# Layer 1 and the FFN read the raw residual; softmax sums are gathered by DMA

## The chip, the cores and the metric

The kernel runs on one core of a Trainium2 chip, as one launch. TensorE (PE, with its weight loads as PEld), VectorE (DVE), ScalarE (ACT), GpSimd (POOL) and the queue of SyncE (SP) work side by side, each on its own list of instructions in order, and wait for one another by semaphores. The metric is the time of the launch on the device in microseconds, as the median of several executions. A profile is one execution.

## What is computed

The input x has 4 images of 128 channels and 64 x 64 pixels, that is 4096 tokens of 128 channels each. Two layers of attention and one recurrent layer (here called the FFN) add to it:

```python
x = x + L0_attention(groupnorm(x))            # q, k of 64 channels, v of 128; softmax over 4096 tokens
t = tokens(x)
t = t + L1_attention(layernorm(t))            # q, k, v of 128; causal; scores * 128**-0.5
t = t + FFN(layernorm(t))
# layernorm(t) = (t - mean) / sqrt(var + 1e-5), over the 128 channels of each token
# FFN: Wx = t @ W.T, normalised per channel over all images and tokens,
#      then y_t = sigmoid(Wx_t + y_{t-1} @ V.T) along the tokens of each image
```

Everything is float32.

## The kernel before

The work is done by `fast_kernel`. (A slower `general_kernel` stands behind it and runs only if a check at the end, written into `wrong`, finds that the recurrence has not converged.) An image is held as X[b], 128 channels on the partitions and 4096 tokens along them. Two of the four images are in SBUF at a time; images 0 and 1 are written to DRAM (`kept`) when they are done and read back at the end.

Attention goes through a list `units`: for each image b, for each layer, for each tile c of 512 queries, for each pair u of key blocks of 128. Layer 0 has 8 tiles of 16 units; layer 1 is causal and has 8 tiles of 2, 4, 6 ... 16 units. `score` (L833) makes the transposed scores `ps` of a unit on TensorE, K blocks as weights, and their exponential `s` on ScalarE (L855 for whole units, L859 for those on the diagonal, which GpSimd then masks, L861). `product` (L867) adds `s` to `total` on VectorE and multiplies it with V on TensorE into `av` (L889). Scores run one unit ahead of products. There are two buffers of `ps`, three of `s`, one of `total`, two of `av`, and two PSUM banks named `misc` for all else.

Around each unit, `step` (L898) advances small generators by one `yield`: all in `ends`, then the first two in `todo`. `whole` runs one to its end where its result is needed.

- `finish` (`e`): after a tile's last unit, the sums in `total` are added, transposed in blocks of 32 and reduced to `part` (128 x 16). A product with `quarters`, `pz`, adds the four quarters of the partitions on TensorE; the reciprocal is spread by a second transpose to `rb`; `o` = `rb` x `av`; `po` = Wv times `o` is added to X.
- `prepare1` (`p1`): layer norm of a tile of 512 tokens for layer 1, in `tokens`: transposed by TensorE, statistics, `rstd` = (var + eps)**-0.5 on GpSimd (L560), then normalised into V1; `back` transposes V1 again into K1, which is both the keys and the source of the queries. `query1` multiplies K1 with M1, a matrix merged from Wq and Wk by `merge1`.
- `ffn` (`f`): the same for the finished residual: `tokens`, `back`, then `pw` = FW times the result, copied into WX, with its statistics in `stats_f`.
- `keys0`, `query0`, `gn_stats`: the inputs of layer 0 for the next image.

`begin_tile` (L796) sets the order: which generators are put into `todo` at which tile, and which are run to their end there. The order within an engine's list isn't always the written one: statistics of image 1 (L595) stand on VectorE from 10.79 us, between steps of image 0, though they are written for the second tile.

After attention, the recurrence runs over 32 positions in 128 chunks at once (L946 to L949), X gets the result on GpSimd (L965), and the images are written out.

Of the kernel before, what the change touches and what calls it, by code (L numbers as in the profile page):

```python
# [472 lines left out]
def fast_kernel(  # L473
# [23 lines left out]

    X = {}

    def load_x(b):  # L500
        X[b] = xpool.tile([P, N], F32, tag=f"X{b % 2}", name=f"X{b}")
        for h in range(8):
            eng = nc.scalar if b == 0 and h % 2 else nc.sync
            eng.dma_start(out=X[b][:, ts(h, N // 8)], in_=x[b, :, ts(h, N // 8)])

    load_x(0)
    load_x(1)
    dram = ctx.enter_context(tc.tile_pool(name="spill", bufs=1, space=bass.MemoryType.DRAM))
    kept = [dram.tile([P, N], F32, name=f"kept{b}") for b in range(B - 2)]

# [41 lines left out]
    stats_f = const.tile([P, B * NQ, 6], F32, name="fstats")  # L552
    M1 = const.tile([P, P], F32, name="M1")

    WX = {}
# [6 lines left out]
    with ExitStack() as actx:  # L562
# [12 lines left out]

        gn, K0, QR, V0, K1, V1, Q = {}, {}, {}, {}, {}, {}, {}


        def merge1():

            pw = misc("pwt")
            nc.tensor.transpose(pw[:, 0:P], W1q, ident)
            nc.tensor.transpose(pw[:, P : 2 * P], W1k, ident)
            wt = tmp.tile([P, 2, P], F32, tag="a", name="wt")
            nc.vector.tensor_copy(wt, pw[:, : 2 * P].rearrange("p (a c) -> p a c", a=2))
            yield
            pm = misc("pm1")
            nc.tensor.matmul(pm[:, :P], lhsT=wt[:, 0, :], rhs=wt[:, 1, :], start=True, stop=True)  # L588
            nc.vector.tensor_copy(M1, pm[:, :P])
            yield  # L590

# [26 lines left out]
        def keys0(b, c):  # L618

            if c == 0:  # L620
                K0[b] = kv.tile([P, N], F32R, tag="K0", name=f"K0_{b}")
                QR[b] = kv.tile([P, N // 2], F32, tag="QR", name=f"QR_{b}")
                V0[b] = wxpool.tile([P, NB, C], F32, tag="V0", name=f"V0_{b}")
            xn = tmp.tile([P, QT], F32, tag="x", name=f"xg_{b}_{c}", bufs=3)
            gmv, grs = gn[b]
# [26 lines left out]
        def query0(b, c):  # L652

            half, col = divmod(c, NQ // 2)
            rows = ds(half * CQ, CQ)
            src = QR[b][rows, ts(col, QT)]
            high = tmp.tile([P, QT], F32, tag="h", name=f"qh_{b}_{c}", bufs=2)
            nc.vector.tensor_scalar(high[rows, :].bitcast(I32), src.bitcast(I32), HIGH, None, ALU.bitwise_and)
            yield
            q = qp.tile([P, 2, QT], F32R, tag="q0", name=f"q0_{b}_{c}")  # L660
            for h in range(2):
                nc.scalar.copy(q[ds(h * CQ, CQ), h, :], high[rows, :])
                nc.vector.tensor_tensor(q[ds((1 - h) * CQ, CQ), h, :], src, high[rows, :], ALU.subtract)  # L663
            Q[b, 0, c] = q
            yield

        def tokens(src, eps, dst, name):

            pt = misc(f"pt_{name}")
            for j in range(4):  # L670
                nc.tensor.transpose(pt[:, ts(j, P)], src[:, ts(j, P)], ident)  # L671
            yield
            stats = small.tile([P, 4, 6], F32, tag="lst", name=f"lst_{name}")
            mv = small.tile([P, 4, 2], F32, tag="lmv", name=f"lmv_{name}")
            for j in range(4):
                nc.vector.bn_stats(stats[:, j, :], pt[:, ts(j, P)])
            for j in range(4):
                nc.vector.bn_aggr(mv[:, j, :], stats[:, j, :])
            rstd = small.tile([P, 4], F32, tag="rstd", name=f"rstd_{name}")
            rsqrt(rstd, mv[:, :, 1], eps, 4)  # L680
            yield
            for j in range(4):
                nc.vector.tensor_scalar(  # L683
                    dst[:, j, :], pt[:, ts(j, P)], mv[:, j, 0:1], rstd[:, j : j + 1],
                    ALU.subtract, ALU.mult,
                )
            yield

        def back(dst, name):
            pb = misc(f"pb_{name}")  # L690
            for j in range(4):
                nc.tensor.transpose(pb[:, ts(j, P)], dst[:, j, :], ident)  # L692
            return pb

        def prepare1(b, c):
            if c == 0:
                K1[b] = kv.tile([P, N], F32, tag="K1", name=f"K1_{b}")
                V1[b] = kv.tile([P, NB, C], F32, tag="V1", name=f"V1_{b}")
            v = V1[b][:, 4 * c : 4 * c + 4, :]
            yield from tokens(X[b][:, ts(c, QT)], 1e-5, v, f"1_{b}_{c}")  # L700
            yield
            pb = back(v, f"1_{b}_{c}")
            nc.scalar.copy(K1[b][:, ts(c, QT)], pb)
            yield

        def query1(b, c):
            pq = misc(f"pq1_{b}_{c}")
            nc.tensor.matmul(pq, lhsT=M1, rhs=K1[b][:, ts(c, QT)], start=True, stop=True)  # L708
            q = qp.tile([P, QT], F32, tag="q1", name=f"q1_{b}_{c}")
            nc.scalar.copy(q, pq)  # L710
            Q[b, 1, c] = q
            yield

        def ffn(b, c):
            if c == 0:
# [3 lines left out]
                )  # L719
            v = tmp.tile([P, 4, C], F32, tag="x", name=f"fv_{b}_{c}", bufs=3)  # L720
            yield from tokens(X[b][:, ts(c, QT)], 1e-5, v, f"f_{b}_{c}")
            if b < len(kept):
                nc.sync.dma_start(out=kept[b][:, ts(c, QT)], in_=X[b][:, ts(c, QT)])
            yield
            pb = back(v, f"f_{b}_{c}")
            xn = tmp.tile([P, QT], F32, tag="x", name=f"fx_{b}_{c}", bufs=3)
            nc.scalar.copy(xn, pb)
            yield
            pw = misc(f"pw_{b}_{c}")
            nc.tensor.matmul(pw, lhsT=FW, rhs=xn, start=True, stop=True)  # L730
            n = QT // CHUNK
            nc.scalar.copy(
                WX[b][:, :, ts(c, n)].rearrange("p l s -> p s l"), pw.rearrange("p (s l) -> p s l", l=CHUNK)
            )
            nc.vector.bn_stats(stats_f[:, b * NQ + c, :], pw)
            yield

        def finish(b, layer, c, av, total):
# [7 lines left out]
            nc.vector.tensor_reduce(part, tt.rearrange("p (k j) -> p k j", j=32), AX.X, ALU.add)  # L746
            yield
            pz = misc(f"pz_{name}")
            nc.tensor.matmul(  # L749
                pz[:, 0:16], lhsT=quarters.rearrange("p a m -> p (a m)"), rhs=part, start=True, stop=True  # L750
            )
            rz = small.tile([P, 16], F32, tag="rz", name=f"rz_{name}")
            nc.vector.reciprocal(rz, pz[:, 0:16])
            rb = tmp.tile([P, 16, 32], F32, tag="a", name=f"rb_{name}")
            nc.vector.transpose(rb, rz.unsqueeze(2).to_broadcast([P, 16, 32]))
            o = tmp.tile([P, QT], F32, tag="b", name=f"o_{name}")
# [6 lines left out]
            xt = X[b][:, ts(c, QT)]  # L763
            nc.vector.scalar_tensor_tensor(xt, po, 1.0 / GUARD, xt, ALU.mult, ALU.add)  # L764
            yield
# [30 lines left out]
        def begin_tile(b, layer, c):  # L796

            if layer == 0:
# [6 lines left out]
                if c == 3 and 0 < b < B - 1:  # L805
                    for k in range(NQ):
                        whole(("f", b - 1, k))
                    load_x(b + 1)
                if c == (5 if b else 1) and b + 1 < B:
                    put(("gn", b + 1), gn_stats(b + 1))  # L810
                whole(("q0", b, c))
                if c + 1 < NQ:
                    put(("q0", b, c + 1), query0(b, c + 1))
            else:
                if c == 0 and b + 1 < B:
                    whole(("gn", b + 1))
                    for k in range(NQ):
                        put(("k0", b + 1, k), keys0(b + 1, k))
                if c == 0:
                    made["q1", b, 0] = after(b, 0)  # L820
                whole(("q1", b, c))
# [11 lines left out]
        def score(i):  # L833
# [11 lines left out]
            for h in range(2):  # L845
                lhsT = (K1 if layer else K0)[b][:, ts(2 * u + h, P)]
                if layer:
# [3 lines left out]
                for k in range(2):  # L851
                    nc.tensor.matmul(ps[:, h, :], lhsT=lhsT, rhs=q[:, k, :], start=k == 0, stop=k == 1)  # L852
            scale, bias = (float(C) ** -0.5, zero) if layer else (1.0, shift)
            if j0 < 0:
                nc.scalar.activation(s, ps, AF.Exp, scale=scale, bias=bias)  # L855
            else:
                for h in range(2):
                    part = s[:, h, first[h] :]
                    nc.scalar.activation(part, ps[:, h, first[h] :], AF.Exp, scale=scale, bias=bias)  # L859
                    edge = s[:, h, ds(first[h], P)]  # L860
# [6 lines left out]
        def product(i):  # L867
# [20 lines left out]
            for h in range(2):  # L888
                nc.tensor.matmul(  # L889
                    av[:, first[h] :], lhsT=V[:, 2 * u + h, :], rhs=s[:, h, first[h] :],  # L890
                    start=u == 0 and h == 0, stop=u == n - 1 and h == 1,
                )
            if u == n - 1:
                key = ("e", b, layer, c)
                made[key] = finish(b, layer, c, av, total)
# [24 lines left out]
    with ExitStack() as fctx:  # L920
# [3 lines left out]
        ps_y = fctx.enter_context(tc.tile_pool(name="ps_y", bufs=1, space=PSUM))  # L924

        for b, k in enumerate(kept):
            X[b] = xback.tile([P, N], F32, name=f"Y{b}")
            for h in range(2):
# [111 lines left out]
```

## Time and profile before

| | |
|---|---|
| median of 3 executions | 2626.08 us (2625.94 to 2628.03) |
| the profiled execution, its own time | 2627.98 us |
| its span, first to last instruction | 2626.1 us |
| granted TensorE clock, mean | 0.991 |
| busy: PE / PEld | 2560.4 / 1398.9 us |
| busy: DVE / ACT / POOL | 1598.5 / 1116.9 / 227.8 us |
| products `av` / scores layer 0 / scores layer 1, on PE | 1466.7 / 763.3 / 501.1 us |
| bytes by DMA | 27.11 MB, 10 GB/s over the span |

How to read it: `L692 PE MATMUL pb<-ident,V ... x128 | 19.2, 272 | 0.0` is a group of instructions by line, engine, operation, output and inputs, with their number, the microseconds that they add to the engine's busy time, the mean nanoseconds of one, and the engine's idle time just before them, with who ended it. A float32 product of 128 x 512 is two TensorE passes and counts twice. A line of the timeline begins with the start and the duration. A DMA row gives the number, the size, and the median microseconds from issue to landing.

### The profile page before, as it was taken

How to read it: one execution, taken by the hardware profiler on the slowest of the kernel's cores; microseconds unless marked ns; L12 is line 12 of the kernel's file. 1: busy time of each engine (PE TensorE's matmuls, PEld its weight loads, DVE VectorE, ACT ScalarE, POOL GpSimd, SP SyncE). 2: the span in 40 equal slices, each digit the busy share in tenths (PEclk: the TensorE clock that was granted, in tenths of full speed). 3: DMA queues.
4: the chain of work that ended last, by engine and by line, in shares of the span. 5: the costliest groups of instructions: out<-in, count | busy, mean ns of one | idle time of the engine just before them, and what ended most of it. 6: DMA issues, size and time to landing. Idle time of an engine off the chain costs nothing.

```text
span 2626.1 us, 21806 instructions
## 1 busy us (share of the span) xinstructions
PE 2560.4 (97%) x7862; PEld 1398.9 (53%) x7862; DVE 1598.5 (61%) x2666; ACT 1116.9 (43%) x1330; POOL 227.8 (9%) x287
## 2 busy tenths in 40 slices
PE   6999999999999999999999999999999999999985
PEld 4555554444555555444555555444455555544454
DVE  6756657654756566655565665675465656654466
ACT  4444444433444444433444444443344444333355
POOL 2100001100000100110000010110000000000016
PEclk9999999999999999999999999999999999999987
DMA  2000000000100000000100000000000000000013
GB/s 71 0 0 1 1 0 12 8 5 4 37 0 0 0 1 5 12 5 8 36 1 1 0 1 1 0 0 1 0 0 1 0 1 1 0 0 1 0 65 130
DMA packets 10501, 27.11 MB, mean 10 GB/s; under 512 B 1936, under 2 KB 2704, under 8 KB 8848
## 3 DMA queue, kind: packets, MB, share of 16 engines
q1 hardware_dynamic: 7488, 19.93, 2.1%
q10 hardware_dynamic: 2896, 5.71, 0.6%
q8 instruction: 63, 1.03, 0.2%
q14 instruction: 54, 0.44, 0.1%
HBM read 13.04 MB, written 12.58 MB: 10 GB/s over the span
## 4 chain that ended last, share of the span: by engine, by line
PE 97%; DVE 2%; DMA 1%; POOL 0%; issue 0%; ACT 0%; POOLq 0%
PE av L889 50%; PE ps L852 18%; PE ps L848 17%; PE py L946 2%; PE po L762 2%; PE pk L632 1%; PE pw L730 1%; PE pq L708 1%; PE pb_f L692 1%; PE pt_f L671 1%; PE pt L671 1%; PE pb L692 1%; PE pt L648 1%; DMA X<-in_x 0%; DVE Y L965 0%; PE pz L749 0%
## 5 line engine op out<-in xcount | busy, mean ns | idle before, releaser
L889 PE MATMUL av<-s,V 128*128 128x512 f32 (+3 forms) x3200 | 1466.7, 580 | 0.0
L882 DVE TENSOR_TENSOR total<-total,s 128x1024 f32<-128x1024 f32 x676 | 826.9, 1223 | 644.1 <-ACT s L855 643.4
L855 ACT ACTIVATE s<-ps,shift 128x1024 f32<-128x1024 f32 x512 | 570.5, 1114 | 785.4 <-PE ps L852 772.9
L889 PEld LDWEIGHTS av<-s,V 128*128 128x128 f32 x3200 | 589.5, 189 | 503.8 <-issue 463.2
L852 PE MATMUL ps<-q,K 128*128 128x512 f32 x2048 | 763.3, 494 | 1.2 <-DVE q L663 1.2
L852 PEld LDWEIGHTS ps<-q,K 128*128 128x128 f32 x2048 | 387.1, 189 | 289.7 <-issue 240.2
L848 PE MATMUL ps<-q,K 128*128 128x512 f32 (+3 forms) x1152 | 501.1, 557 | 0.0
L855 ACT ACTIVATE s<-ps,zero 128x1024 f32<-128x1024 f32 x224 | 249.6, 1114 | 477.5 <-PE ps L848 470.3
L848 PEld LDWEIGHTS ps<-q,K 128*128 128x128 f32 x1152 | 216.0, 190 | 240.8 <-issue 229.1
L560 POOL TENSOR_TENSOR rstd<-rstd,mhalf 128x4 f32<-128x4 f32 x32 | 33.1, 1034 | 1212.6 <-DVE rstd L559 1212.6
L859 ACT ACTIVATE s<-ps,zero 128x512 f32<-128x512 f32 (+3 forms) x128 | 60.6, 524 | 105.5 <-PE ps L848 105.5
L886 DVE TENSOR_TENSOR total<-total,s 128x256 f32<-128x256 f32 (+1 forms) x120 | 57.5, 498 | 72.2 <-POOL s L861 72.2
L861 POOL TENSOR_SCALAR_AFFINE_SELECT s<-s 128x128 f32<-128x128 f32 x128 | 45.6, 367 | 451.7 <-ACT s L859 450.6
L629 POOL TENSOR_SCALAR X<-X,B0v 128x512 f32<-128x512 f32 x32 | 63.0, 1972 | 145.7 <-DVE xg L627 145.7
L764 DVE SCALAR_TENSOR_TENSOR X<-po,X 128x512 f32<-128x512 f32 x64 | 44.2, 690 | 49.4 <-PE po L762 49.0
L560 POOL TENSOR_TENSOR rstd_f<-rstd_f,mhalf 128x4 f32<-128x4 f32 x32 | 32.7, 1023 | 475.8 <-DVE rstd_f L559 475.8
L683 DVE TENSOR_SCALAR V<-pt,lmv,rstd 128x128 f32<-128x128 f32 x128 | 44.0, 404 | 36.6 <-POOL rstd L560 36.6
L683 DVE TENSOR_SCALAR fv<-pt_f,lmv_f,rstd_f 128x128 f32<-128x128 f32 x128 | 44.0, 403 | 30.8 <-POOL rstd_f L560 30.8
L948 DVE SCALAR_TENSOR_TENSOR z<-WX,fgain,py 128x128 f32<-128x128 f32 (+1 forms) x176 | 56.6, 347 | 4.6 <-PE py L946 0.5
L880 DVE COPY total<-s 128x1024 f32<-128x1024 f32 (+2 forms) x68 | 43.6, 642 | 17.4 <-ACT s L855 10.0
L663 DVE TENSOR_TENSOR q<-QR,qh 64x512 fp32r<-64x512 f32 x64 | 43.9, 686 | 7.2 <-PE ps L852 6.5
L742 DVE TENSOR_TENSOR t<-total 128x512 f32<-128x512 f32 x64 | 44.3, 692 | 4.4 <-PE pm L588 2.3
(112 smaller groups left out, 1323.3 us busy)
## 6 DMA issues: line engine op xcount, KB each, us to landing
X<-in_x SPq DMA_DIRECT2D x28, 256.0 KB, 4.8
kept<-X SPq DMA_DIRECT2D x16, 256.0 KB, 2.0
Y<-kept SPq DMA_DIRECT2D x4, 1024.0 KB, 8.0
out<-Y SPq DMA_DIRECT2D x2, 1024.0 KB, 8.0
out<-Y ACTq DMA_DIRECT2D x2, 1024.0 KB, 8.5
out<-X SPq DMA_DIRECT2D x2, 1024.0 KB, 16.3
out<-X ACTq DMA_DIRECT2D x2, 1024.0 KB, 16.9
X<-in_x ACTq DMA_DIRECT2D x4, 256.0 KB, 5.7
```

The lines of the kernel that those rows point to most:

```text
L560: nc.gpsimd.tensor_tensor(dst, dst, mhalf[:, :n], ALU.pow)
L629: nc.gpsimd.tensor_scalar(xt, xt, B0v, None, ALU.add)
L671: nc.tensor.transpose(pt[:, ts(j, P)], src[:, ts(j, P)], ident)
L683: nc.vector.tensor_scalar(dst[:, j, :], pt[:, ts(j, P)], mv[:, j, 0:1], rstd[:, j : j + 1], ALU.subtract, ALU.mult,)
L848: nc.tensor.matmul(ps[:, h, first[h] :], lhsT=lhsT, rhs=q[:, first[h] :], start=True, stop=True)
L852: nc.tensor.matmul(ps[:, h, :], lhsT=lhsT, rhs=q[:, k, :], start=k == 0, stop=k == 1)
L855: nc.scalar.activation(s, ps, AF.Exp, scale=scale, bias=bias)
L859: nc.scalar.activation(part, ps[:, h, first[h] :], AF.Exp, scale=scale, bias=bias)
L882: nc.vector.tensor_tensor(total, total, s, ALU.add)
L886: nc.vector.tensor_tensor(t, t, s[:, h, first[h] :], ALU.add)
L889: nc.tensor.matmul(av[:, first[h] :], lhsT=V[:, 2 * u + h, :], rhs=s[:, h, first[h] :], start=u == 0 and h == 0, stop=u == n - 1 and h == 1,)
L948: nc.vector.scalar_tensor_tensor(z[:, :n], w, gain, ps[:, :n], ALU.mult, ALU.add)
```

## The change

In layer 1 and in the FFN, TensorE reads the raw residual. `merge1` centres Wq, Wk and FW over the input channels (`center`), so that the mean of a token falls out of the products; FW is turned back into `FWc`. The deviation of a key is then a factor of its row of scores: `R1` is the per-partition scale of the exponential, which is therefore issued once for each block of 128 keys and no longer once for a pair. The deviation of a query, or of an FFN token, is a factor of its column: `deviations` writes `rstd` to DRAM as a row of 512, and `spread` reads that row back to all 128 partitions. The second transposes (`back`), K1 and the FFN's normalised tile are gone; V1 stays as it was. As X is read as keys all through layer 1, its result goes to a new buffer X2; three images instead of two are kept in DRAM.

In `finish`, `part` goes to DRAM and comes back as 32 partitions x 4 quarters, is added and inverted on VectorE, goes to DRAM as a row of 512, and is read back to all partitions. The very last tile keeps `pz`. All pending `ends` are run to their end when a tile's last product is issued. The load of image 1 is put behind the fifth unit, by a GpSimd copy into it that waits for `total`. q of both layers share two buffers; `xg` has two instead of three.

```diff
+    def load_x(b, behind=None):
         X[b] = xpool.tile([P, N], F32, tag=f"X{b % 2}", name=f"X{b}")
+        if behind is not None:
+            nc.gpsimd.tensor_copy(X[b].rearrange("p (h n) -> p h n", h=8)[:, :, 0], behind)
...
-    load_x(1)
...
+        def center(dst, src, n):
+            m = small.tile([P, n], F32, tag="cm", name="cm")
+            nc.vector.tensor_reduce(m, src, AX.X, ALU.add)
+            nc.vector.tensor_scalar(m, m, 1.0 / P, None, ALU.mult)
+            for k in range(n):
+                nc.vector.tensor_scalar(dst[:, k, :], src[:, k, :], m[:, k : k + 1], None, ALU.subtract)
 
         def merge1():
...
+            nc.tensor.transpose(pw[:, 2 * P : 3 * P], FW, ident)
+            wt = tmp.tile([P, 3, P], F32, tag="a", name="wt")
+            center(wt, pw[:, : 3 * P].rearrange("p (a c) -> p a c", a=3), 3)
...
+            pf = misc("pfw")
+            nc.tensor.transpose(pf[:, :P], wt[:, 2, :], ident)
+            nc.vector.tensor_copy(FWc, pf[:, :P])
...
-        def tokens(src, eps, dst, name):
+        def deviations(src, eps, name):
...
             rsqrt(rstd, mv[:, :, 1], eps, 4)
+            row = dram.tile([4, P], F32, tag=f"row_{name}", name=f"row_{name}")
+            nc.sync.dma_start(out=row.rearrange("j p -> p j"), in_=rstd)
+            rows[name] = row
+            return pt, mv, rstd
+
+        def spread(name, tag, bufs):
+            rb = tmp.tile([P, QT], F32, tag=tag, name=f"rb_{name}", bufs=bufs)
+            row = rows.pop(name).rearrange("(o j) p -> o (j p)", o=1)
+            nc.sync.dma_start(out=rb, in_=row.to_broadcast([P, QT]))
+            return rb
...
-            pb = back(v, f"1_{b}_{c}")
-            nc.scalar.copy(K1[b][:, ts(c, QT)], pb)
...
         def query1(b, c):
+            rb = spread(f"1_{b}_{c}", "rq", 1)
+            yield
+            yield
             pq = misc(f"pq1_{b}_{c}")
-            nc.tensor.matmul(pq, lhsT=M1, rhs=K1[b][:, ts(c, QT)], start=True, stop=True)
-            q = qp.tile([P, QT], F32, tag="q1", name=f"q1_{b}_{c}")
-            nc.scalar.copy(q, pq)
+            nc.tensor.matmul(pq, lhsT=M1, rhs=X[b][:, ts(c, QT)], start=True, stop=True)
+            q = qp.tile([P, 2, QT], F32, tag="q", name=f"q1_{b}_{c}")[:, 0, :]
+            nc.vector.scalar_tensor_tensor(q, pq, float(C) ** -0.5, rb, ALU.mult, ALU.mult)
...
-            pb = back(v, f"f_{b}_{c}")
-            xn = tmp.tile([P, QT], F32, tag="x", name=f"fx_{b}_{c}", bufs=3)
-            nc.scalar.copy(xn, pb)
+            deviations(src, 1e-5, f"f_{b}_{c}")
+            rb = spread(f"f_{b}_{c}", "r", 2)
...
-            nc.tensor.matmul(pw, lhsT=FW, rhs=xn, start=True, stop=True)
+            nc.tensor.matmul(pw, lhsT=FWc, rhs=src, start=True, stop=True)
+            w = tmp.tile([P, QT], F32, tag="w", name=f"w_{b}_{c}")
+            nc.vector.tensor_tensor(w, pw, rb, ALU.mult)
...
+                there = dram.tile([P, 16], F32, tag="there", name=f"there_{name}", bufs=2)
+                nc.sync.dma_start(out=there, in_=part)
+                side = small.tile([32, 4, 16], F32, tag="side", name=f"side_{name}")
+                nc.sync.dma_start(out=side, in_=there.rearrange("(q j) k -> j q k", q=4))
+                yield
+                yield
+                z = small.tile([32, 16], F32, tag="z", name=f"z_{name}")
+                nc.vector.tensor_reduce(z, side.rearrange("j q k -> j k q"), AX.X, ALU.add)
+                nc.vector.reciprocal(z, z)
+                row = dram.tile([16, 32], F32, tag="zrow", name=f"zrow_{name}", bufs=2)
+                nc.sync.dma_start(out=row.rearrange("k j -> j k"), in_=z)
+                nc.sync.dma_start(
+                    out=rb.rearrange("p k j -> p (k j)"),
+                    in_=row.rearrange("(o k) j -> o (k j)", o=1).to_broadcast([P, QT]),
+                )
+                yield
+                yield
...
-                if c == (5 if b else 1) and b + 1 < B:
+                if c == (5 if b else 2) and b + 1 < B:
                     put(("gn", b + 1), gn_stats(b + 1))
+                if c == NQ - 1:
+                    put(("q1", b, 0), after(b, 0))
...
+            for h in range(2 if layer else 0):
+                part = s[:, h, first[h] :]
+                scale = R1[b][:, 2 * u + h : 2 * u + h + 1]
+                nc.scalar.activation(part, ps[:, h, first[h] :], AF.Exp, scale=scale, bias=zero)
...
+            if (b, layer, c, u) == (0, 0, 0, 4):
+                load_x(1, total[:, 0, 0:8])
             if u == n - 1:
+                for key in list(ends):
+                    whole(key)
```

More of the change, by code (lines that the diff above doesn't have):

```diff
@@ L495, in fast_kernel @@
     wxpool = ctx.enter_context(tc.tile_pool(name="wx", bufs=1))
-    X = {}
-    def load_x(b):
+    X, X2 = {}, {}
+    def load_x(b, behind=None):
         X[b] = xpool.tile([P, N], F32, tag=f"X{b % 2}", name=f"X{b}")
+        if behind is not None:
+            nc.gpsimd.tensor_copy(X[b].rearrange("p (h n) -> p h n", h=8)[:, :, 0], behind)
         for h in range(8):
@@ L506, in fast_kernel @@
     load_x(0)
-    load_x(1)
-    dram = ctx.enter_context(tc.tile_pool(name="spill", bufs=1, space=bass.MemoryType.DRAM))
-    kept = [dram.tile([P, N], F32, name=f"kept{b}") for b in range(B - 2)]
+    dram = ctx.enter_context(tc.tile_pool(name="dram", bufs=1, space=bass.MemoryType.DRAM))
+    kept = [dram.tile([P, N], F32, name=f"kept{b}") for b in range(B - 1)]
     def load(src, shape, name):
@@ L553, in fast_kernel @@
     M1 = const.tile([P, P], F32, name="M1")
+    FWc = const.tile([P, P], F32, name="FWc")
     WX = {}
@@ L574, in misc @@
             return ps_m.tile([P, QT], F32, tag="m", name=name)
-        gn, K0, QR, V0, K1, V1, Q = {}, {}, {}, {}, {}, {}, {}
+        gn, K0, QR, V0, V1, Q, rows, R1 = {}, {}, {}, {}, {}, {}, {}, {}
+        def center(dst, src, n):
[4 more added lines that the diff above has]
+                nc.vector.tensor_scalar(dst[:, k, :], src[:, k, :], m[:, k : k + 1], None, ALU.subtract)
         def merge1():
@@ L583, in merge1 @@
             nc.tensor.transpose(pw[:, P : 2 * P], W1k, ident)
-            wt = tmp.tile([P, 2, P], F32, tag="a", name="wt")
-            nc.vector.tensor_copy(wt, pw[:, : 2 * P].rearrange("p (a c) -> p a c", a=2))
+            nc.tensor.transpose(pw[:, 2 * P : 3 * P], FW, ident)
+            wt = tmp.tile([P, 3, P], F32, tag="a", name="wt")
+            center(wt, pw[:, : 3 * P].rearrange("p (a c) -> p a c", a=3), 3)
             yield
@@ L623, in keys0 @@
                 V0[b] = wxpool.tile([P, NB, C], F32, tag="V0", name=f"V0_{b}")
-            xn = tmp.tile([P, QT], F32, tag="x", name=f"xg_{b}_{c}", bufs=3)
+            xn = tmp.tile([P, QT], F32, tag="x", name=f"xg_{b}_{c}", bufs=2)
             gmv, grs = gn[b]
@@ L658, in query0 @@
             nc.vector.tensor_scalar(high[rows, :].bitcast(I32), src.bitcast(I32), HIGH, None, ALU.bitwise_and)
-            yield
-            q = qp.tile([P, 2, QT], F32R, tag="q0", name=f"q0_{b}_{c}")
+            q = qp.tile([P, 2, QT], F32R, tag="q", name=f"q0_{b}_{c}")
             for h in range(2):
@@ L671, in tokens @@
                 nc.tensor.transpose(pt[:, ts(j, P)], src[:, ts(j, P)], ident)
-            yield
             stats = small.tile([P, 4, 6], F32, tag="lst", name=f"lst_{name}")
@@ L680, in tokens, with prepare1 @@
             rsqrt(rstd, mv[:, :, 1], eps, 4)
-            yield
+            row = dram.tile([4, P], F32, tag=f"row_{name}", name=f"row_{name}")
[7 more added lines that the diff above has]
+            return rb
+        def prepare1(b, c):
+            if c == 0:
+                V1[b] = kv.tile([P, NB, C], F32, tag="V1", name=f"V1_{b}")
+                R1[b] = small.tile([P, NB], F32, tag="R1", name=f"R1_{b}")
+            pt, mv, rstd = deviations(X[b][:, ts(c, QT)], 1e-5, f"1_{b}_{c}")
+            nc.gpsimd.tensor_copy(R1[b][:, ts(c, 4)], rstd)
             for j in range(4):
                 nc.vector.tensor_scalar(
-                    dst[:, j, :], pt[:, ts(j, P)], mv[:, j, 0:1], rstd[:, j : j + 1],
+                    V1[b][:, 4 * c + j, :], pt[:, ts(j, P)], mv[:, j, 0:1], rstd[:, j : j + 1],
                     ALU.subtract, ALU.mult,
@@ L687, in tokens, with query1 @@
             yield
[L689 to L700, printed above, removed]
+        def query1(b, c):
+            rb = spread(f"1_{b}_{c}", "rq", 1)
             yield
-            pb = back(v, f"1_{b}_{c}")
-            nc.scalar.copy(K1[b][:, ts(c, QT)], pb)
             yield
-        def query1(b, c):
             pq = misc(f"pq1_{b}_{c}")
-            nc.tensor.matmul(pq, lhsT=M1, rhs=K1[b][:, ts(c, QT)], start=True, stop=True)
-            q = qp.tile([P, QT], F32, tag="q1", name=f"q1_{b}_{c}")
-            nc.scalar.copy(q, pq)
+            nc.tensor.matmul(pq, lhsT=M1, rhs=X[b][:, ts(c, QT)], start=True, stop=True)
+            q = qp.tile([P, 2, QT], F32, tag="q", name=f"q1_{b}_{c}")[:, 0, :]
+            nc.vector.scalar_tensor_tensor(q, pq, float(C) ** -0.5, rb, ALU.mult, ALU.mult)
             Q[b, 1, c] = q
@@ L719, in ffn @@
                 )
-            v = tmp.tile([P, 4, C], F32, tag="x", name=f"fv_{b}_{c}", bufs=3)
-            yield from tokens(X[b][:, ts(c, QT)], 1e-5, v, f"f_{b}_{c}")
+            src = X2[b][:, ts(c, QT)]
             if b < len(kept):
-                nc.sync.dma_start(out=kept[b][:, ts(c, QT)], in_=X[b][:, ts(c, QT)])
+                nc.sync.dma_start(out=kept[b][:, ts(c, QT)], in_=src)
             yield
-            pb = back(v, f"f_{b}_{c}")
-            xn = tmp.tile([P, QT], F32, tag="x", name=f"fx_{b}_{c}", bufs=3)
-            nc.scalar.copy(xn, pb)
+            deviations(src, 1e-5, f"f_{b}_{c}")
+            rb = spread(f"f_{b}_{c}", "r", 2)
+            yield
             yield
             pw = misc(f"pw_{b}_{c}")
-            nc.tensor.matmul(pw, lhsT=FW, rhs=xn, start=True, stop=True)
+            nc.tensor.matmul(pw, lhsT=FWc, rhs=src, start=True, stop=True)
+            w = tmp.tile([P, QT], F32, tag="w", name=f"w_{b}_{c}")
+            nc.vector.tensor_tensor(w, pw, rb, ALU.mult)
             n = QT // CHUNK
             nc.scalar.copy(
-                WX[b][:, :, ts(c, n)].rearrange("p l s -> p s l"), pw.rearrange("p (s l) -> p s l", l=CHUNK)
+                WX[b][:, :, ts(c, n)].rearrange("p l s -> p s l"), w.rearrange("p (s l) -> p s l", l=CHUNK)
             )
-            nc.vector.bn_stats(stats_f[:, b * NQ + c, :], pw)
+            nc.vector.bn_stats(stats_f[:, b * NQ + c, :], w)
             yield
@@ L746, in finish @@
             nc.vector.tensor_reduce(part, tt.rearrange("p (k j) -> p k j", j=32), AX.X, ALU.add)
[L747 to L753, printed above, removed]
-            rb = tmp.tile([P, 16, 32], F32, tag="a", name=f"rb_{name}")
-            nc.vector.transpose(rb, rz.unsqueeze(2).to_broadcast([P, 16, 32]))
+            rb = tmp.tile([P, 16, 32], F32, tag="a", name=f"rb_{name}")
+            if (b, layer, c) == (B - 1, 1, NQ - 1):
+                yield
+                pz = misc(f"pz_{name}")
+                nc.tensor.matmul(
+                    pz[:, 0:16], lhsT=quarters.rearrange("p a m -> p (a m)"), rhs=part, start=True, stop=True
+                )
+                rz = small.tile([P, 16], F32, tag="rz", name=f"rz_{name}")
+                nc.vector.reciprocal(rz, pz[:, 0:16])
+                nc.vector.transpose(rb, rz.unsqueeze(2).to_broadcast([P, 16, 32]))
+            else:
+                there = dram.tile([P, 16], F32, tag="there", name=f"there_{name}", bufs=2)
[12 more added lines that the diff above has]
+                    in_=row.rearrange("(o k) j -> o (k j)", o=1).to_broadcast([P, QT]),
+                )
+                yield
+                yield
             o = tmp.tile([P, QT], F32, tag="b", name=f"o_{name}")
@@ L763, in finish @@
             xt = X[b][:, ts(c, QT)]
-            nc.vector.scalar_tensor_tensor(xt, po, 1.0 / GUARD, xt, ALU.mult, ALU.add)
+            if layer and c == 0:
+                X2[b] = xpool.tile([P, N], F32, tag="X2", name=f"X2_{b}")
+            dst = X2[b][:, ts(c, QT)] if layer else xt
+            nc.vector.scalar_tensor_tensor(dst, po, 1.0 / GUARD, xt, ALU.mult, ALU.add)
             yield
@@ L818, in begin_tile @@
                         put(("k0", b + 1, k), keys0(b + 1, k))
-                if c == 0:
-                    made["q1", b, 0] = after(b, 0)
                 whole(("q1", b, c))
@@ L845, in score @@
             for h in range(2):
-                lhsT = (K1 if layer else K0)[b][:, ts(2 * u + h, P)]
+                lhsT = (X if layer else K0)[b][:, ts(2 * u + h, P)]
                 if layer:
@@ L852, in score @@
                     nc.tensor.matmul(ps[:, h, :], lhsT=lhsT, rhs=q[:, k, :], start=k == 0, stop=k == 1)
[L853 to L859, printed above, removed]
+            if not layer:
+                nc.scalar.activation(s, ps, AF.Exp, bias=shift)
+            for h in range(2 if layer else 0):
+                part = s[:, h, first[h] :]
+                scale = R1[b][:, 2 * u + h : 2 * u + h + 1]
+                nc.scalar.activation(part, ps[:, h, first[h] :], AF.Exp, scale=scale, bias=zero)
+                if j0 >= 0:
                     edge = s[:, h, ds(first[h], P)]
@@ L924, in fast_kernel @@
         ps_y = fctx.enter_context(tc.tile_pool(name="ps_y", bufs=1, space=PSUM))
+        X[B - 1] = X2[B - 1]
         for b, k in enumerate(kept):
-            X[b] = xback.tile([P, N], F32, name=f"Y{b}")
+            X[b] = xpool.tile([P, N], F32, tag="X0", name="Y0") if b == 0 else xback.tile([P, N], F32, name=f"Y{b}")
             for h in range(2):
```

## The prediction

> **What bounds the kernel now.** I read the page's slices and chain first, then stretches of the span, then TensorE's own groups and waits, then time order around one change of layer.
>
> ```profile
> PE   6999999999999999999999999999999999999985
> PEclk9999999999999999999999999999999999999987
> ...
> PE 97%; DVE 2%; DMA 1%; POOL 0%; issue 0%; ACT 0%; POOLq 0%
> ```
>
> TensorE is the chain, at full clock, except in the first and the last two slices. The stretches say how full it is (start and end, length, then busy time of PE, PEld, DVE, ACT, POOL; clock, DMA share, GB/s):
>
> ```profile
> 27.00:388.00 361.00, 361.00 (x1149) 208.76 (x1150) 227.71 (x325) 166.52 (x170) 20.27 (x15) 1.00 0.00 1
> 388.00:655.00 267.00, 266.34 (x748) 129.34 (x747) 159.34 (x292) 108.41 (x138) 28.22 (x43) 1.00 0.02 7
> 2513.40:2551.60 38.20, 26.10 (x119) 20.47 (x119) 26.12 (x88) 20.00 (x53) 1.55 (x2) 0.73 0.27 110
> ```
>
> Between 27 and 2513 us the eight attention stretches leave TensorE idle for about 3 us in all. So there TensorE work that goes is time that goes, microsecond for microsecond, and a new wait is time only if it is longer than the work queued ahead of it. VectorE and ScalarE have a third of the time free. TensorE's groups, shapes apart:
>
> ```profile
> L692 PE MATMUL pb_f<-ident,fv 128*128 128x128 f32 x128 | 20.0, 275 | 3.0 <-DVE fv L683 3.0
> L692 PE MATMUL pb<-ident,V 128*128 128x128 f32 x128 | 19.2, 272 | 0.0
> L749 PE MATMUL pz<-part,quarters 128*128 128x16 f32 x128 | 18.7, 222 | 1.7 <-DVE part L746 1.7
> ```
>
> The busy column (20.0, 19.2, 18.7) is what they add to TensorE; the mean of one overlaps its neighbours.
>
> **What goes from TensorE.** K1 and the FFN input are no longer turned back: 19.2 + 20.0 = 39.2 us. The small product `pz` goes in 63 of 64 tiles: 18.7 x 63/64 = 18.4 us. `merge1` gains one 128x128 transpose before and one after centring, at 0.27: +0.5. Scores, `pq`, `pw`, `po` and the transposes that feed the statistics stay, in the same shapes. Net -57.1 us.
>
> **What moves on the other engines.** VectorE loses the FFN's `fv` (44.0), 63 transposes `rb` of about 0.7 and gains `q` and `w` (64 of about 0.69, the row of `o`), 63 four-way sums (bounded by 0.16 and 0.68, the smallest row and the reduce `part`; 0.25) and the centring (under 2 us): about -25 us. ScalarE loses the copies L703, L710, L727 (18.5 + 18.6 + 18.8) and splits 224 exps: two of 128x512 at 0.687 for one at 1.114, so +58. Scale by a column instead of a constant is in no row; I take the same duration; were it longer by the shortest ScalarE row, 0.36, the 448 halves would take 161 us more on an engine that waits 470 us for scores in that layer. Cover is the unit of 3.43 us of TensorE against 1.4 of exp. POOL gets 32 small copies. All this I cost at nothing.
>
> **The start.** The second image's load goes behind the fifth unit. In time order of the first 20 us its statistics stand on VectorE between the steps of the first image's own: `dev` could start at 11.8 and starts at 12.83, its square waits 1.6 more, then 1.05 and 0.8: 4.5 us. ScalarE's issue of weights and its table load end at 18.65 while `k` starts at 21.13, so 2.5 us go even if that queue doesn't move. Bounds 0 and 5; I take -3.5. The displaced statistics run later on an idle VectorE.
>
> **The new transfers.** In 63 tiles the sum goes SBUF to DRAM (128 x 64 B), back to 32 partitions, then as a row of 512 pieces of 4 B to DRAM, then spread to 128 partitions (256 KB). The trace shows:
>
> ```profile
> kept<-X SPq DMA_DIRECT2D x16, 256.0 KB, 2.0
> ...
> B0v<-in_b0v ACTq DMA_DIRECT2D x1, 0.5 KB, 4.9
> Fgamma<-in_fgamma ACTq DMA_DIRECT2D x1, 0.5 KB, 2.7
> Fbeta<-in_fbeta ACTq DMA_DIRECT2D x1, 0.5 KB, 2.4
> ```
>
> Quiet queue: 2.0 for 256 KB. `Fbeta` is 128 pieces of 4 B. No row has 512 such pieces: between 2.0 and four times the slowest, 19.6; nearest is `Fbeta`, and I take 3.5. The other three: 2.2 each (2.0 to 4.9). Chain from `part` to `o` done: 2.2 + 2.2 + 0.5 (sum, reciprocal 0.26) + 3.5 + 2.2 + 0.69 = 11.3 us, where before `pz` to `o` took 2.05 (397.69 to 399.74).
> [...] With 2.0 for all four that chain would be 9.2.
>
> **Where the chain is not covered.** A finish is stepped once per unit, two steps for each pair of transfers: 5.3 us of TensorE in layer 0 (units 2.64 apart by the starts of `total`), 6.9 in layer 1. The pair takes 4.4 or 5.7, so in tiles of six units or more it is covered. VectorE waits in order at the four-way sum and at `o`; behind them stand `total` adds, and three `s` buffers give TensorE two units before it feels that. The tight place is where layer 1 begins with tiles of two and four units:
>
> ```profile
> 388.82 0.69 DVE L742 TENSOR_TENSOR t<-total 128x512 f32<-128x512 f32 x1
> ...
> 390.32 0.66 DVE L746 TENSOR_REDUCE part<-tt 128x16 f32<-128x512 f32 x1
> ...
> 399.05 0.69 DVE L757 SCALAR_TENSOR_TENSOR o<-rb,av 128x512 f32<-128x512 f32 x1
> ```
> ```profile
> 402.43 1.88 PE L889 MATMUL av<-s,V 128*128 128x512 f32 x4
> ...
> 417.75 1.88 PE L889 MATMUL av<-s,V 128*128 128x512 f32 x4
> ```
>
> There are two `av` banks, so the first product of the four-unit tile (402.43) needs the `o` of layer 0's last tile: 391.0 + 0.1 + 11.3 = 402.4, a wait of about nothing. If the added loop over `ends` pins `po` where it is written, after the two-unit tile (its last `av` ends near 399.4), TensorE stands 3 us. The next finish can't begin before `rb`'s buffer is free: `part` at 404.5, `o` at 415.8, needed at 417.75. So 0 to 3 us per image: 2.5 x 4 = 10. By the chain at all upper ends (4.9 + 4.9 + 0.5 + 19.6 + 4.9 + 0.7 = 35.5) each of the two waits grows by 24 us: 190 us for four images.
> Behind the same SP queue stand `load_x` (two of them just as a finish starts; 8 x 0.32 us of issue and 2 MB): bounds 0 and 10 each, 2 x 2 = 4. Rows for 64 statistics and their spreads share SP too; `w` and `q` wait for them on VectorE two steps later, and misc PSUM has two banks: in layer 1, 0 to 4 us per image by bounds of one late transfer, 1.5 x 4 = 6. Together +20 (0 to about 220).
> A wait may cost more than itself. After 1.8 us of idle at 2517 the two `po` passes took 2.08 for the 1.02 they take at 401, with the clock of that stretch at 0.73; TensorE had waited before too. [...]
>
> **The tail.** The last finish keeps its path. Its FFN: `rstd` done at 2524.4, then row 3.5, spread 2.2, `w` 0.69, statistics 0.69, so 2531.7 with gaps, where `fstats` ended at 2530.9: +1. With 2.0 + 2.0 it is -1, with 19.6 + 4.9 it is +18. One more image comes back from DRAM: four 1 MB loads issued at 2513.5 landed about 10 us later, so six are there before 2555.7, when POOL first needs one.
>
> **Sum.** -57.1 - 3.5 + 20 + 1 = -39.6. The profiled execution took 2627.98 (span 2626.1 and 1.9 around it): 2588.4. It lies 1.9 above the median of the runs, 2626.08, so 2587 (2586.5).
>
> **Rivals.**
> 1. All waits are hidden: -57.1 - 3.5 + 1 gives 2566. For: covers of 402.4 against 402.43. Against: that cover leaves nothing.
> 2. The change of layer is the new bound, and it is slower. Place: products of the second and third tile of layer 1 wait for `o`. Each microsecond above 11.3 in the chain costs 2 per image, 8 in all; 39.6 are there to lose, so from 16.3 us on, transfers of 3.8 on the mean against 2.5. At 5.0 the chain is 21.2: 2587 + 79 = 2666; from 2621 on. For: 4.4 to 4.9 in rows of small loads, and an untried 512-piece one. Against: those ran beside 4 MB of input.
> 3. A little at every joint: 63 finishes and 64 rows cost 0.3 us more each (VectorE standing in front of QR and `xg`): 127 x 0.3 = 38, about 2625: the same.
> 4. It doesn't do what it says: the check at the end starts the second, general kernel; more than twice the time.
>
> **How the numbers follow.** 0.2% (5 us) is about what a measurement can tell. Forecast 0.57, in its own range 2571 to 2612 (waits of 4 to 45 us); rival 1 0.14; rival 3 0.07; rival 2 0.20; rival 4 0.02. Faster 0.57 + 0.14 = 0.71, same 0.07, slower 0.22. The range goes from 2562, just under rival 1 with a start gain of 5 and a tail of -1, to 2645, into rival 2: about 0.15 lies outside, nearly all above.
>
> **What would show it.** L692 gone and `pz` once; busy TensorE near 2503; first score near 23 us; landings of 2 to 2.5, and of 3 to 4 for 4-byte rows; TensorE's waits for `o` about 10 us, four times near the change of layer. Wrong if the 4-byte rows land after 5 us or more, if `total` waits for transfers long enough that ScalarE lacks `s` buffers, or if TensorE's clock drops mid-run.

## The result, and the profile after

| | before | after |
|---|---|---|
| median | 2627.06 us | 3094.59 us |
| ratio after / before | | 1.176, interval 1.171 to 1.182 |
| span of the profiled execution | 2626.1 us | 3090.6 us |
| mean granted TensorE clock | 0.991 | 0.930 |
| TensorE busy / not busy | 2560.4 / 65.7 us | 2681.1 / 409.5 us |

The forecast was 2587 in a range of 2562 to 2645; the kernel became 467 us slower. The span grew by 464.5: TensorE stood still 344 us longer, and what it did took 121 us longer, though work had been taken from it. The page of the changed kernel shows it in its slices: 21 of 40 now read 8 or less in TensorE's row, where all but three read 9 before, and the clock reads 8 in places in the middle, where it was 9 throughout.

```profile
PE   8899989779899998978889998977889999788955
...
PEclk9999999889899999989999999998999999888977
```

The DMA view of the changed kernel has the new transfers (number, KB each, median us from issue to landing). For the four transfers of the gather, what was taken as 2.2, 2.2, 3.5 and 2.2 us is 1.4, 1.6, 6.2 and 3.6; the rows of deviations, of 512 pieces as well, take 8.3 and 8.4.

```profile
rb<-zrow SPq DMA_DIRECT2D x63, 256.0 KB, 3.6
rb<-row SPq DMA_DIRECT2D x32, 256.0 KB, 3.3
rb_f<-row_f SPq DMA_DIRECT2D x32, 256.0 KB, 4.8
...
there<-part SPq DMA_DIRECT2D x63, 8.0 KB, 1.4
side<-there SPq DMA_DIRECT2D x63, 8.0 KB, 1.6
zrow<-z SPq DMA_DIRECT2D x63, 2.0 KB, 6.2
row<-rstd SPq DMA_DIRECT2D x32, 2.0 KB, 8.3
row_f<-rstd_f SPq DMA_DIRECT2D x32, 2.0 KB, 8.4
```

Who waits for them stands in the view of waits (engine and line, what it waited for: total us, times, longest):

```profile
DVE o L798 <- DMA rb<-zrow: 378.8, 62, 11.9
ACT WX L753 <- DVE w L751: 345.1, 32, 27.8
DVE w L751 <- DMA rb_f<-row_f: 282.4, 27, 16.6
...
PE po L803 <- DVE o L798: 151.9, 46, 9.7
...
PE av L933 <- ACT s L902: 133.3, 25, 9.3
```

VectorE stands 379 us before `o` and 282 before `w`. TensorE meets the first through `po`, and the second by a longer way: `WX`, the copy of `w`, stands in ScalarE's list ahead of the exps, and the products wait for those. The time order of one ordinary tile of layer 0 shows the first way whole (start, duration, engine; in brackets the idle time before and who ended it):

```profile
1066.20 0.24 DVE L788 RECIPROCAL z<-z 32x16 f32<-32x16 f32 x1
...
1066.46 0.32 SPq L790 DMA_DIRECT2D zrow<-z  x1
...
1067.38 1.50 PE L896 MATMUL ps<-q,K 128*128 128x512 f32 x4
1067.42 1.23 DVE L926 TENSOR_TENSOR total<-total,s 128x1024 f32<-128x1024 f32 x1 [0.98 <-ACT s L898]
...
1070.07 1.22 DVE L926 TENSOR_TENSOR total<-total,s 128x1024 f32<-128x1024 f32 x1 [1.42 <-ACT s L898]
...
1072.52 0.34 SPq L791 DMA_DIRECT2D rb<-zrow  x1
...
1076.54 0.69 DVE L798 SCALAR_TENSOR_TENSOR o<-rb,av 128x512 f32<-128x512 f32 x1 [5.25 <-DMA rb<-zrow]
1077.14 1.22 DVE L926 TENSOR_TENSOR total<-total,s 128x1024 f32<-128x1024 f32 x1
...
1077.28 2.08 PE L803 MATMUL po<-o,W0v 128*128 128x512 f32 x2 [3.10 <-DVE o L798]
...
1079.14 3.62 PE L933 MATMUL av<-s,V 128*128 128x512 f32 x4
```

`o` stands two additions behind the reciprocal. VectorE is there at 1071.3, the row lands at 1076.5. `po` stands in TensorE's list where `o` was thought to be done: TensorE idles 3.10 us. Then it is slow: `po` takes 2.08 us where it takes 1.02 undisturbed (in the kernel before, below), the next four passes 3.62 instead of 1.88.

```profile
401.14 1.02 PE L762 MATMUL po<-o,W0v 128*128 128x512 f32 x2
```

Before the `po` of layer 0 TensorE idles 102.5 us in all.

The second way, in layer 1 of the second image, while rows of its FFN are prepared:

```profile
1298.67 2.02 SPq L699 DMA_DIRECT2D row_f<-rstd_f  x1
...
1301.86 0.23 DVE L788 RECIPROCAL z<-z 32x16 f32<-32x16 f32 x1
...
1308.48 0.32 SPq L707 DMA_DIRECT2D rb_f<-row_f  x1
1308.90 0.38 SPq L790 DMA_DIRECT2D zrow<-z  x1
1309.38 0.43 SPq L707 DMA_DIRECT2D rb<-row  x1
1313.57 0.69 DVE L751 TENSOR_TENSOR w<-pw,rb_f 128x512 f32<-128x512 f32 x1 [10.40 <-DMA rb_f<-row_f]
1314.18 1.22 DVE L926 TENSOR_TENSOR total<-total,s 128x1024 f32<-128x1024 f32 x1
1314.30 1.08 ACT L753 COPY WX<-w 128x512 f32<-128x512 f32 x1 [12.35 <-DVE w L751]
1315.19 2.75 ACT L902 ACTIVATE s<-ps,zero,R 128x512 f32<-128x512 f32 x4
...
1315.99 3.78 PE L933 MATMUL av<-s,V 128*128 128x512 f32 x4 [7.37 <-ACT s L902]
```

ScalarE stands 12.35 us at `WX` with finished scores behind it, and TensorE 7.37. `z` had been ready at 1302.1 (its reciprocal ends there), but its row leaves only at 1308.90: SyncE is one list too, and stood at `rb_f` until the row ahead of it had landed.

### The profile page after: what moved, and what is told of

The parts are those of the page before. It is cut to its first block, busy times and chain, and to the rows that moved or that the text cites. A ratio compares the mean times of both kernels' runs of the same rounds, so it can differ in the third digit from the quotient of the medians.

```text
span 3090.6 us, 21916 instructions
## 1 busy us (share of the span) xinstructions
PE 2681.1 (87%) x7482; PEld 1412.6 (46%) x7482; DVE 1556.7 (50%) x2607; ACT 1148.1 (37%) x1458; POOL 237.9 (8%) x320
## 5 line engine op out<-in xcount | busy, mean ns | idle before, releaser
L933 PE MATMUL av<-s,V 128*128 128x512 f32 (+3 forms) x3200 | 1555.5, 611 | 179.1 <-ACT s L902 133.3
L933 PEld LDWEIGHTS av<-s,V 128*128 128x128 f32 x3200 | 628.0, 200 | 770.9 <-issue 504.7
L902 ACT ACTIVATE s<-ps,zero,R 128x512 f32<-128x512 f32 (+1 forms) x576 | 391.5, 737 | 485.4 <-PE ps L892 459.6
L896 PEld LDWEIGHTS ps<-q,K 128*128 128x128 f32 x2048 | 392.5, 192 | 298.9 <-issue 248.4
L892 PE MATMUL ps<-q,X 128*128 128x512 f32 (+3 forms) x1152 | 516.9, 574 | 3.8 <-ACT s L902 1.9
L892 PEld LDWEIGHTS ps<-q,X 128*128 128x128 f32 x1152 | 227.1, 200 | 271.2 <-issue 250.1
L798 DVE SCALAR_TENSOR_TENSOR o<-rb,av 128x512 f32<-128x512 f32 x64 | 44.0, 688 | 378.9 <-DMA rb<-zrow 378.8
L753 ACT COPY WX<-w 128x512 f32<-128x512 f32 x32 | 34.6, 1080 | 345.1 <-DVE w L751 345.1
L803 PE MATMUL po<-o,W0v 128*128 128x512 f32 x64 | 58.3, 1009 | 102.5 <-DVE o L798 102.5
L803 PE MATMUL po<-o,W1v 128*128 128x512 f32 x64 | 43.7, 771 | 50.3 <-DVE o L798 49.4
```

The source lines that it names most:

```text
L803: nc.tensor.matmul(po, lhsT=W1v if layer else W0v, rhs=o, start=True, stop=True)
L892: nc.tensor.matmul(ps[:, h, first[h] :], lhsT=lhsT, rhs=q[:, first[h] :], start=True, stop=True)
L933: nc.tensor.matmul(av[:, first[h] :], lhsT=V[:, 2 * u + h, :], rhs=s[:, h, first[h] :], start=u == 0 and h == 0, stop=u == n - 1 and h == 1,)
```

## The experiments

Three theories. A: the reads `o` and `w` stand earlier in VectorE's list than their transfers land, and block TensorE through `po` and through the exps. B: SyncE's queue has too many transfers. C: layer 1's exps, split and scaled by a column, are the new bound. Four kernels tell them apart. They were run once each, beside one run of the kernel before at 2627.9; the four executions of the changed kernel lie within 26 us (3072.95 to 3099.04), far less than the differences read here.

**Softmax sums by `pz` again.**

```diff
+            yield
+            pz = misc(f"pz_{name}")
...
             rb = tmp.tile([P, 16, 32], F32, tag="a", name=f"rb_{name}")
-            if (b, layer, c) == (B - 1, 1, NQ - 1):
-                yield
-                pz = misc(f"pz_{name}")
...
-                there = dram.tile([P, 16], F32, tag="there", name=f"there_{name}", bufs=2)
...
+            nc.vector.transpose(rb, rz.unsqueeze(2).to_broadcast([P, 16, 32]))
```

(`wt` in `merge1` moves to another buffer, to stay out of the way of `rb`.)

> The changed kernel, with the softmax sums made by pz on TensorE again in all 64 tiles; the rows for queries and FFN still go through DRAM. Theory A (the two reads o and w stand in VectorE's order earlier than their transfers land, and block TensorE through po and through the exps): the 152 us that TensorE waits for o go, with most of the slow clock after them, and pz comes back for 18: 2820 to 2900 us. Theory B (SyncE's queue is crowded, each transfer late because it stands behind others): 252 of its 423 transfers go, so the waits for FFN rows collapse as well: 2590 to 2680. Theory C (layer 1's exps, split and with a column as scale, are the new bound): no change beyond pz, 3050 to 3110.

Measured: 2807.0 us, clock 0.963. Just under A's range, far from B and C. With 252 transfers fewer on SyncE the wait for FFN rows stayed as it was (289 us before `w`), and TensorE still waits for the exps, 107 us (83.8 in layer 1, below, and 22.9 in layer 0). `rb_f` takes 4.7 us to land, as with the crowd.

```profile
DVE w L751 <- DMA rb_f<-row_f: 289.3, 29, 16.1
PE av L913 <- ACT s L882: 83.8, 19, 7.3
```

**Fewer pieces, as many transfers.**

```diff
-                nc.sync.dma_start(out=row.rearrange("k j -> j k"), in_=z)
+                nc.vector.transpose(zt, z)
+                nc.sync.dma_start(out=row, in_=zt[0:16, :])
...
-            nc.sync.dma_start(out=row.rearrange("j p -> p j"), in_=rstd)
+            nc.tensor.transpose(pr[0:4, 0:P], rstd, ident)
+            nc.vector.tensor_copy(rt, pr[0:4, 0:P])
+            nc.sync.dma_start(out=row, in_=rt)
```

> The changed kernel, but the rows are turned before they are written: z by a 32x32 transpose on VectorE, so that it goes out as 16 pieces of 128 B, rstd by a small TensorE transpose, so that it goes out as 4 pieces of 512 B, in place of 512 pieces of 4 B each. As many transfers on the same queue, same bytes. Theory A: the writes land in about 2 us instead of 6.2 and 8.3; the wait for o (5.25 us in an ordinary tile) shrinks to about 1, that for w by 6 of 10: 2640 to 2760 us, of which about 10 us are the 64 new transposes. Theory B (number of transfers): 3000 or more. Theory C: 3050 to 3110.

Measured: 2629.6 us beside 2627.9 of the kernel before, clock 0.990. More than A expected; B and C fall. The waits of this kernel:

```profile
PE pr_f L700 <- POOL rstd_f L563: 14.9, 22, 2.6
...
PE po L810 <- DVE o L805: 6.8, 5, 1.8
```

TensorE's wait for `o` is 6.8 us instead of 151.9. The profile has no landing times for these transfers, but SyncE issues the spread when the row has landed: 1.2 us after the last FFN row (2524.00 to 2525.18), where from row to spread the 512 pieces take 8.4 in the changed kernel. VectorE's wait for the spread before `o` is 68.8 us instead of 378.8. TensorE's longest wait in the middle of the kernel is now for the repair itself: the new small transpose `pr_f` stands before GpSimd has done the power.

**The same transfers, read later.** `o` and `w` come three steps later, and an order edge on VectorE puts them behind the latest addition to `total`.

```diff
+                yield
+                yield
+                yield
...
-            nc.vector.scalar_tensor_tensor(
+            with tc.issue_after(behind["add"]):
+                nc.vector.scalar_tensor_tensor(
...
+            with tc.issue_after(behind["add"]):
+                nc.vector.tensor_tensor(w, pw, rb, ALU.mult)
...
-                nc.vector.tensor_tensor(total, total, s, ALU.add)
+                behind['add'] = nc.vector.tensor_tensor(total, total, s, ALU.add).ins
```

> The changed kernel, transfers as they are, but o and w are ordered on VectorE behind more additions to total (o by two more units, w by three steps more). Theory A: in layer 0 o is due about when the row lands (10.6 us after z), w about 17 us after its row was started: 2640 to 2780 us, the first tiles of layer 1 keep their waits. Theory B: lateness depends on the queue and stays: gain below 100, 2990 or more. Theory C: 3050 to 3110.

Measured: 2728.9 us, clock 0.974. With every 4-byte row as slow as before (6.1, 8.3, 8.3), 366 of the 467 us come back. That is A's range, and neither C nor the B of the expectation. What is left is 76 us of TensorE's waits for `o`, of 16 tiles instead of 46, a late start of the recurrence (22.6 us of TensorE's waiting, as in the change, against 4.9 in the kernel before), and a clock still below that kernel's.

```profile
PE po L812 <- DVE o L807: 76.2, 16, 8.8
```

**The gather alone, on the kernel before.** The diff is the new branch of `finish` and the loop over `ends`.

> The kernel before, with only the gathered softmax sums added (and the loop that runs pending ends to their end). Theory A: 63 times about 3 us of waiting and 2 us of slow clock, less 18 us of pz: 2800 to 2950 us. Theory B: only its own four transfers for each tile are on SyncE, no crowd: 2600 to 2650. Theory C: layer 1's exps are as before, so 2610 to 2640.

Measured: 2840.3 us, clock 0.967; `zrow` lands after 6.1, VectorE waits 347 us before `o`, TensorE 153 before `po`. A again: with no other transfer near it, the chain of four costs 212 us net.

```profile
DVE o L777 <- DMA rb<-zrow: 346.7, 63, 10.6
...
PE po L782 <- DVE o L777: 153.2, 44, 7.1
```

So A is shown from both sides: landing sooner or reading later each takes most of the loss away. B as it was stated is not the cause. A smaller part remains open. The FFN's and the queries' rows alone cost 2807.0 - 2596.6 = 210 us (the 2596.6 is the same kernel with both remedies, below), the gather alone 2840.3 - 2627.9 = 212, or 215 with the 3 that it gains when mended, and both 3094.6 - 2593.5 = 501. Some 75 us are left that neither part has alone. TensorE's waits for `o` do not hold them: 153 us alone, 152 together. ScalarE's before `WX` grow from 300 to 345 when the gather is added, and TensorE's for the exps from 107 to 154. Two things could make `w` later still: it stands behind a waiting `o` in VectorE's list, and rows and spreads stand behind one another in SyncE's, as the z row did that left 7 us late. No run separates the two.

**Both remedies, and the price of the work removed.** The rows are turned by block transposes on VectorE, nothing on TensorE; rstd leaves in four transfers.

```diff
+            nc.gpsimd.memset(wide[:, 4:32], 1.0)
...
-            nc.sync.dma_start(out=row.rearrange("j p -> p j"), in_=rstd)
+            nc.vector.transpose(rt, wide)
+            for h in range(4):
+                nc.sync.dma_start(out=row[:, ts(h, 32)], in_=rt[ds(32 * h, 4), :])
```

with the z transpose of the second kernel, and `o` and `w` two steps later, again by an order edge.

> The changed kernel with both remedies: z and rstd are turned by block transposes on VectorE and written in pieces of 128 B (rstd by four transfers of 4 partitions each, so more transfers than before, and nothing added on TensorE); o and w stand two steps later on VectorE. Theory A (late landing is all that it lost): the waits go, and what is left is the TensorE work removed and the earlier start. Priced by the time that the removed instructions took from one start to the next (0.43 for four transposes, 0.14 for one pz: 27.5 + 8.8 = 36) and 5 for the start: 2585 to 2605 us. Priced by the busy column as in the prediction (57): 2565 to 2580. Theory B (number of transfers on SyncE, here 192 more): slower than the run with pieces, 2640 or more.

Measured: 2593.45 us against 2628.1, ratio 0.987 (0.985 to 0.989): faster than both kernels, with 192 more transfers than the change has. It is the change with its rows made quick to land and its readers put later. TensorE's busy time falls by 44.9 us against the kernel before, the span by 35.2: it is idle 75.4 us instead of 65.7, of which the start of the recurrence takes 14.9 instead of 4.9.

The same with `pz`:

```diff
-                there = dram.tile([P, 16], F32, tag="there", name=f"there_{name}", bufs=2)
...
+            nc.vector.transpose(rb, rz.unsqueeze(2).to_broadcast([P, 16, 32]))
```

> As the run before this one, but the softmax sums by pz on TensorE in all tiles. Theory A with the start-to-start price: 27.5 and 5 saved, few waits: 2594 to 2610 us, within 10 us of the run with both remedies, that is, the gather is worth no more than 9. By the busy column: 18 slower than that run.

Measured: 2596.56 us, 0.988 (0.987 to 0.990). The two intervals overlap: once the rows are mended, the gather is worth about 3 us, which is within the intervals, though each of the four times here (2596.42 to 2597.54) is above each of the four there (2592.70 to 2594.15). TensorE is busy 13.7 us less with it (2529.2 to 2515.5), and about 10 are given back in idle time.

The kernel before without the second transposes, which leaves layer norm out of the queries, the keys and the FFN's input, and so gives another result:

```diff
-            pb = back(v, f"1_{b}_{c}")
-            nc.scalar.copy(K1[b][:, ts(c, QT)], pb)
+            nc.scalar.copy(K1[b][:, ts(c, QT)], X[b][:, ts(c, QT)])
...
-            pb = back(v, f"f_{b}_{c}")
...
-            nc.scalar.copy(xn, pb)
+            nc.scalar.copy(xn, X[b][:, ts(c, QT)])
```

> The kernel before with the second transposes (pb, pb_f; 64 times four) left out and no transfer added: K1 and the FFN's input are copied from the unnormalised X, so layer norm is left out of the queries, the keys and the FFN's input. It prices the removed TensorE work alone. Start-to-start price: 64 x 0.43 = 27.5 less, 2596 to 2602 us. Busy column: 39.2 less, 2585 to 2590 us.

Measured: 2594.78 us, 33.3 less than before (ratio 0.9875, 0.9858 to 0.9893). It lies between the two prices and outside both ranges. The page's row of busy times gives the same number: TensorE's total falls from 2560.4 to

```profile
PE 2527.1 (98%) x7606; PEld 1370.9 (53%) x7606; DVE 1597.0 (62%) x2666; ACT 1121.2 (43%) x1330; POOL 227.5 (9%) x287
```

that is, by 33.3, while the groups had said 39.2.

Last, the kernel with both remedies splits the loss of the change, because both have the same 7482 instructions on TensorE in the trace. The change first, then the mended kernel:

```profile
PE 2681.1 (87%) x7482; PEld 1412.6 (46%) x7482; DVE 1556.7 (50%) x2607; ACT 1148.1 (37%) x1458; POOL 237.9 (8%) x320
PE 2515.5 (97%) x7482; PEld 1356.3 (52%) x7482; DVE 1576.9 (61%) x2734; ACT 1158.1 (45%) x1458; POOL 255.1 (10%) x447
```

The spans are 3090.6 and 2590.9. The same work takes 165.6 us longer in the change, and TensorE is idle 409.5 instead of 75.4 us: 165.6 + 334.1 = 499.7, the difference of the spans. The granted clock can account for the first term: its mean is 0.930 over the 3090.6 us of the change and 0.991 over the 2590.9 of the mended kernel, and 0.070 x 3090.6 - 0.009 x 2590.9 = 193 is the most that slower passes could add; TensorE was idle in a part of that time.

## Why the prediction was wrong

- **"In tiles of six units or more it is covered."** This is the step that failed. The working set a pair of transfers (4.4 or 5.7) against two steps (5.3 in layer 0) and called it covered; the second pair was over its cover by its own numbers. Measured, the pair `zrow` and `rb` takes 9.8. Behind a read that comes too early I counted only what waits for buffers ("two units before it feels that"). But `po` stands in TensorE's own list at a place fixed before the run, and no `s` buffer helps: of VectorE's 379 us before `o`, 152 reached TensorE through `po`, in 46 waits. The bound was 0 to 220 us for a few tiles at the change of layer, when it should have been a price for all 63.
- **The 4-byte row at 3.5.** It was 6.2 and 8.3, inside the bounds of 2.0 to 19.6 but far from the row called nearest (`Fbeta`, 128 pieces). The spread `rb`, set at 2.2 after the `kept` row, was 3.3 to 4.8. The 8 KB transfers here, of 128 pieces of 64 B, land after 1.4 and 1.6, and 2 KB in 512 pieces takes 6.2 or more, so here the pieces decide and not the bytes.
- **The rows of deviations at 1.5 us an image.** About 210 us in all, FFN and queries together. The step named VectorE as the one that waits, and stopped there: behind `w` stood ScalarE's copy into WX, behind that the exps, behind those the products. ScalarE's list was counted as a third free and its order was not looked at.
- **No term for the clock.** The sum adds nothing for it, which was the author's estimate and which no run shows; the runs show 165.6 us more for the same passes, a third of the loss. In the tile shown the clock falls 2.15 us into the wait of 3.10 and stays at half for 6.83 (stretch, length, then busy time of PE, PEld, DVE, ACT, POOL; clock, DMA share, GB/s):

  ```profile
  1074.17:1076.32 2.15, 0.00 (x1) 0.00 (x0) 0.00 (x0) 1.11 (x1) 0.00 (x0) 1.00 0.65 115
  1076.32:1083.15 6.83, 5.88 (x8) 2.69 (x9) 3.65 (x4) 0.00 (x0) 0.00 (x0) 0.50 0.00 1
  1083.15:1090.00 6.85, 6.85 (x26) 4.18 (x25) 3.59 (x11) 2.56 (x3) 0.54 (x1) 1.00 0.00 0
  ```

  The prediction's own row had hinted at it, with slow passes after 1.8 us at 2517, and was set aside. Here half of the 5.88 us worked at half speed is lost, 2.9, about as much again as the wait. Over the whole kernel it is half as much again, 165.6 beside 334.
- **-57.1 us of TensorE work.** The measured figures are 33.3 for the transposes and 13.7 for `pz`, about 47. I said that the busy column is what a group adds to TensorE. It is not: the rows of a group overlap those of their neighbours too, as four transposes at 402.00 that last 0.60 with the next product at 402.43 show. The mechanism was right and the size off by a sixth.
- **The start, -3.5.** The first scores came at 21.13 instead of 26.78, 5.7 us, just beyond the bound of 5. **The tail, +1** was about +10 (from the end of the last `av` to the first `z`, 19.8 before and 29.6 after): the last FFN row left at 2975.98 and its spread at 2987.55, 11.6 us later where 8.4 is usual, with loads of Y on the same queue, and `w` waited 16.6 us. I had priced the row at 3.5 and the loads at nothing.
- **Split exps and the column scale at nothing.** Right for the time: the mended kernels have the same exps without the waits. The sizes were off, though: a column as scale makes the exp of 128x512 last 0.77 us and not 0.69, and ScalarE gained 31 us of busy time where the prediction's terms gave 2.
- **Rival 2** ended on the right side, but neither its place nor its condition was as put. The mean landing was (1.4 + 1.6 + 6.2 + 3.6) / 4 = 3.2, below the 3.8 from which it was to decide. As a chain, its 16.3 us were just met in the tile shown (`part` ends at 1060.98, `o` at 1077.23: 16.25). And layer 0's tiles, which it left out, hold 102.5 of the 151.9 us of waiting before `po`.
- **Its own signs.** Of the three signs of being wrong that the prediction named, two came: 4-byte rows land after more than 5 us, and the clock drops in mid-run.

## What to carry to other kernels

A transfer that replaces a few hundred nanoseconds of TensorE puts its reader into an in-order list at a place chosen before the run. Ask of each reader what stands behind it on its engine, and again behind that, up to the engine that bounds; the depth of the buffers says nothing of a wait that stands in the bounding engine's own list. Write a row for broadcasting in a few long pieces, turned on chip first, and read it later: here that made the change 1.3% faster instead of 17.6% slower. Nearly all of the gain comes from the second transposes; the gather is worth about 3 us at best. The busy column of a group overstates what its removal is worth (39.2 for 33.3), the time from start to start understated it (27.5); a run without the group, read by the engine's total, gave the price.

## What the runs showed of the hardware

- A DRAM write of 2 KB in 512 pieces of 4 B landed after 6.2 us (from 32 partitions) or 8.3 to 8.4 (from 128). With one kind alone on the queue it is the same: 6.1 for the gather alone, 8.4 for the rows alone. With 16 pieces of 128 B the next transfer could leave 1.4 us after (1017.21 to 1018.59 in the kernel with both remedies). Why the same 512 pieces take 2 us longer from 128 partitions than from 32 stays open.
- In the changed kernel the granted clock fell 71 times, from 1.00 to 0.50, 436 us in all at half speed; in the kernel before it stayed at 1.00 from 30 to 2460 us. The falls of this trace lie whole multiples of 3.41 us apart. In the 3.41 us ahead of each TensorE was idle for 1.94 us or more in sum, and after the first 70 us no other such stretch at full clock has more than 1.93; the ends of passes are modelled, so the last tenths are not sure. Of the 71 stretches at half speed 32 lasted 3.41 us and 32 lasted 6.83.
- An exp with a column as scale took 0.08 to 0.09 us longer than one with a constant, at each of four sizes: 0.77 us for 128x512 in the mean against 0.69 (32 on the diagonal), 0.45 against 0.36 for 128x128.
